# A four-layer convolution and state-space kernel: token stage under the kernel's own list schedule, side work on ScalarE, first convolution in three bf16 parts

## The chip, the cores and the metric

The kernel runs on one core of a Trainium2 chip. The time is that of the device in microseconds (us), the median of several runs. The profile is one execution taken by the hardware profiler. Engines are called PE (TensorE), DVE (VectorE), ACT (ScalarE), POOL (GpSimd) and SP (SyncE, which here only issues DMAs). All arithmetic is fp32 unless said otherwise.

## What is computed

The input x is 64 images of 128 channels and 28x28 pixels. Four layers follow each other; each works on the output of the one before:

```
# layer 0: quantised residual block
out = conv3x3(x, quant_weight(w1, 4))          # weights: integers -15..15, over 15
out = quant_act(batchnorm(out, gamma1, beta1), 4)
out = conv3x3(out, quant_weight(w2 * (mask2 > 0.5), 4))
x   = quant_act(batchnorm(out, gamma2, beta2) + x, 4)
# layer 1: self-attention over the 784 pixels of an image
x   = gamma * (softmax(q^T k) applied to v) + x
# layer 2: state-space scan over 784 steps (160 channels x 24 states), fused back, residual
x   = x + scale * (fusion_w @ mamba(layernorm(four scan directions of x)))
# layer 3: state-space scan over 8 tokens of 16 channels for each pixel (32 channels x 16 states)
seq = x.transpose(0, 2, 3, 1).reshape(B * H * W, 8, 16)
  xz = seq @ in_proj_w.T ; causal conv of width 4, silu -> xs ; B, C, dt from xs
  dt = softplus(dt * dt_proj_w + dt_proj_b)
  h  = exp(dt_t * A) * h + dt_t * B_t * xs_t ;  y_t = sum over 16 states of h * C_t
  out = ((y + xs * D) * silu(z)) @ out_proj_w.T
x   = x + silu(groupnorm(out, 4 groups))
```

Batch norm in layer 0 takes its mean and variance over all 64 images, so the first convolution must be finished before the second can start.

## The kernel before, in words

The work has three parts, one after the other, joined by tensors in DRAM.

**conv_block (lines 135 to 213)** runs the two convolutions. Weights are quantised once by `quantised` (line 147): `q1`, the first convolution's, as fp32, and `q2` as bf16. Then a loop over 32 groups of two images loads `xt` (line 177), and `conv3x3` (line 116) makes for each image and each half of it nine matmuls that accumulate in one PSUM bank, one for each tap of the 3x3 window (line 126). For the first convolution both operands are fp32. ACT copies the sums out (line 182), DVE takes batch statistics (line 184), and the result goes to DRAM. The second loop reads it back, quantises it to integers in bf16 (`qa`, line 199) and does the same with bf16 operands. These two loops are written in program order, and the framework's scheduler, which simulates the engines' time, orders the instructions of each engine.

**attention_and_mamba (from line 491)** does layers 1 and 2. It doesn't issue its instructions where they are written. A `Plan` (line 259) records each of them as a step, with the tiles it uses and the steps it must follow; a helper class makes one line, 472, issue all of them, so that in the profile they all have the line L472. `Plan.cost` (line 365) gives each step a price: for a matmul 0.06 + 0.0023 us per column, for POOL 0.2 + 0.0023 per element, for ACT 0.2 + 0.00093 per element, for DVE 0.14 + 0.00107 per element (tensor_scalar in SBUF 0.00053). POOL's steps, and those DVE steps that read two SBUF operands or are a tensor_scalar into SBUF, are marked as sharing one port, of which the planner lets one run at a time. `order` (line 392) is a list scheduler: it walks through simulated time and takes for each engine, among its first 32 ready steps, the first that can start within `patience` of the soonest. Steps recorded under `first()` get an earlier rank by `lead`. `issue` (line 466) tries twelve pairs of lead and patience, takes the order that ends first by its own prices, and issues it as a fixed order. Steps recorded under `together()` stay side by side.

**token_mamba (from line 1077)** does layer 3. Before the change it issues directly, and the framework's scheduler orders it. The 50,176 pixels are cut into 28 groups of 14x128; each group has two halves of 16 channels (`dh`), each half four blocks of four channels, so there are 224 blocks. For each:

- `x_proj` (once a group): matmuls L1192 and L1198 give B, C and dt; the pairs of columns are copied out of PSUM into `BC` at L1202; `small` holds dt and the sum over states of B*C (L1207 to L1216).
- `delta_u` (once a half): ACT makes `delta`, PE transposes `u`; softplus is built from ACT's Abs, Exp and Ln, with DVE's L1254 (w = e + 1), L1255 and L1256 and POOL's L1259 and L1260; L1263 makes `diag`.
- `exps` (once a block): 64 small ACT exponentials, 128x98 each, fill the tile `a` of one block. There are two such tiles.
- `block`: POOL makes `db` = u*B for each token (`inject`, L1293; five tiles), and L1304 and L1306; DVE carries the state `h` in PSUM over the tokens: L1305, then L1308 (h*a), L1310 (h*C, written over `a`, or into `late` for the last two tokens) and L1312 (h + db). PE sums over the 16 states with identity matmuls: L1315, L1317 (which reads `a`, and so frees it) and L1319. ACT copies the sum into `ysb`.
- `gate` (once a half): PE transposes back, L1335 adds D*u, L1336 multiplies by z on POOL, a DRAM tensor `ygd` holds the first half until the second is there, L1344 projects, L1354 copies into the image's tile `xr`.
- `finish_image` (once an image, 64 in all): group norm statistics (L1137, L1139), ten tiny operations on a 128x8 tile `sm` (L1143 to L1154, mostly on DVE, with an Ln and an Exp on ACT), a silu gate by three ACT operations, the affine xr at L1162 on DVE, and on POOL L1164 and L1165.

All ACT operations of this part that go through `tables.act` have the line L228. The driver loop at the end of the function interleaves the parts: in each block it advances the gate and finish steps of the half before by two, the next group's `x_proj` by two and the next half's `delta_u` by one, and issues the next block's exps ahead of the present block.

Of the kernel before, what the change touches and what calls it, by code (L numbers as in the profile page):

```python
# [16 lines left out]
F32 = mybir.dt.float32  # L17
# [98 lines left out]
def conv3x3(nc, ps, w, src):  # L116

    img = src.rearrange("p (h w) -> p h w", w=HW)
    taps = [(0, 0)] + [(dy, dx) for dy in (-1, 0, 1) for dx in (-1, 0, 1) if (dy, dx) != (0, 0)]
    for half in range(2):  # L120
        acc = ps[:, half, :HT].rearrange("p (h w) -> p h w", w=HW)
        r0 = half * 14
        for i, (dy, dx) in enumerate(taps):
            lo, hi = max(r0, -dy), min(r0 + 14, HW - dy)
            a, b = max(0, -dx), min(HW, HW - dx)
            nc.tensor.matmul(  # L126
                acc[:, lo - r0 : hi - r0, a:b],
                lhsT=w[:, (dy + 1) * 3 + dx + 1, :],
                rhs=img[:, lo + dy : hi + dy, a + dx : b + dx],
                start=(i == 0),  # L130
                stop=(i == len(taps) - 1),
            )


def conv_block(tc, cpool, dram, x, w1t, w2t, m2t, v, eps):
# [6 lines left out]
    with ExitStack() as ctx:  # L142
# [4 lines left out]
        def quantised(name, src, mask, dtype):  # L147
# [19 lines left out]
            q = wp.tile([C, 9, C], dtype, name=f"q{name}")  # L167
# [3 lines left out]
        q1 = quantised("1", w1t, None, F32)  # L171
        q2 = quantised("2", w2t, m2t, BF16)

        st1 = wp.tile([C, NB * 2, 6], F32, name="st1")
        for g in range(NB // GRP):
            xt = big.tile([C, GRP, T], F32, name="xt")
            nc.sync.dma_start(xt, x[g * GRP : (g + 1) * GRP].rearrange("b c t -> c b t"))
            raw = big.tile([C, GRP, T], F32, name="raw")
            for k in range(GRP):
                acc = ps.tile([C, 2, 512], F32, name="acc")  # L180
                conv3x3(nc, acc, q1, xt[:, k, :])
# [10 lines left out]
        for g in range(NB // GRP):  # L192
# [7 lines left out]
            for k in range(GRP):  # L200
                acc = ps.tile([C, 2, 512], F32, name="acc")
                conv3x3(nc, acc, q2, qa[:, k, :])
# [56 lines left out]
class Plan:  # L259
# [12 lines left out]
    def __init__(self, tc):  # L272
        self.tc = tc
# [91 lines left out]
    def cost(self, engine, method, outs, ins, args, kw):  # L365
# [5 lines left out]
        if engine == "tensor":  # L371
# [4 lines left out]
            return 0.06 + 0.0023 * n, False, 0.25  # L376
        if engine == "gpsimd":
            return 0.2 + 0.0023 * n, True, 0.07
# [112 lines left out]
def attention_and_mamba(tc, tables, x, c2d, s2, b2x15, x2d, utd, ztd, pk3, pk4, vec, v, ident, eps):  # L491
# [11 lines left out]
    with ExitStack() as ctx:  # L503
# [99 lines left out]
        plan = Plan(tc)  # L603
# [473 lines left out]
def token_mamba(tc, tables, x2d, utd, ztd, pk4, v, ident, eps, out, NB):  # L1077
# [17 lines left out]
    with ExitStack() as ctx:  # L1095
        dram = ctx.enter_context(dram)
        wp = ctx.enter_context(tc.tile_pool(name="w4", bufs=1))
# [3 lines left out]
        ap = ctx.enter_context(tc.tile_pool(name="a4", bufs=2))  # L1101
        p2 = ctx.enter_context(tc.tile_pool(name="p4", bufs=2))
        p1 = ctx.enter_context(tc.tile_pool(name="p4b", bufs=1))
        db = ctx.enter_context(tc.tile_pool(name="db4", bufs=5))
        cp = ctx.enter_context(tc.tile_pool(name="c4", bufs=4))
        xrp = ctx.enter_context(tc.tile_pool(name="xr4", bufs=4))
        ps = ctx.enter_context(tc.tile_pool(name="ps4", bufs=3, space=PSUM))
        psd = ctx.enter_context(tc.tile_pool(name="psd4", bufs=1, space=PSUM))
        psh = ctx.enter_context(tc.tile_pool(name="psh4", bufs=1, space=PSUM))
        psy = ctx.enter_context(tc.tile_pool(name="psy4", bufs=2, space=PSUM))  # L1110
# [13 lines left out]
        act = tables.act  # L1124
        act(A, w("Alog"), AF.Exp)
        nc.vector.tensor_scalar(A, A, -1.0, None, ALU.mult)

# [5 lines left out]
        def finish_image(b):  # L1133
            xo = xr.pop(b)
            stats = p2.tile([C, 2, 6], F32, name="stats")
            for h in range(2):
                nc.vector.bn_stats(stats[:, h, :], xo[:, h * HT : (h + 1) * HT])  # L1137
            mv = p2.tile([C, 2], F32, name="mv")
            nc.vector.bn_aggr(mv, stats.rearrange("p n s -> p (n s)"))  # L1139
            acc = bank()  # L1140
            nc.tensor.matmul(acc[:, 0:1], lhsT=grp, rhs=mv[:, 0:1], start=True, stop=True)
            sm = p2.tile([C, 8], F32, name="sm", bufs=4)
            nc.vector.tensor_copy(sm[:, 0:1], acc[:, 0:1])  # L1143
            nc.vector.tensor_sub(sm[:, 1:2], mv[:, 0:1], sm[:, 0:1])
            nc.vector.scalar_tensor_tensor(sm[:, 2:3], sm[:, 1:2], sm[:, 1:2], mv[:, 1:2], ALU.mult, ALU.add)
            acc2 = bank()
            nc.tensor.matmul(acc2[:, 0:1], lhsT=grp, rhs=sm[:, 2:3], start=True, stop=True)
            act(sm[:, 3:4], acc2[:, 0:1], AF.Ln, bias=eps)
            act(sm[:, 4:5], sm[:, 3:4], AF.Exp, scale=-0.5)
            nc.vector.tensor_mul(sm[:, 5:6], sm[:, 4:5], v("gn_gamma"))  # L1150
            nc.vector.tensor_mul(sm[:, 6:7], sm[:, 0:1], sm[:, 5:6])
            nc.vector.tensor_sub(sm[:, 7:8], v("gn_beta"), sm[:, 6:7])
            nc.vector.tensor_scalar(sm[:, 0:1], sm[:, 5:6], -1.0, None, ALU.mult)
            nc.vector.tensor_scalar(sm[:, 1:2], sm[:, 7:8], -1.0, None, ALU.mult)  # L1154
            res = p1.tile([C, T], F32, name="res")
            nc.sync.dma_start(res, x2d[b])

            e = p1.tile([C, T], F32, name="gate")
            act(e, xo, AF.Exp, bias=sm[:, 1:2], scale=sm[:, 0:1])
            act(e, e, AF.Ln, bias=1.0)  # L1160
            act(e, e, AF.Exp, scale=-1.0)
            nc.vector.tensor_scalar(xo, xo, sm[:, 5:6], sm[:, 7:8], ALU.mult, ALU.add)  # L1162
            yield
            nc.gpsimd.tensor_tensor(xo, xo, e, ALU.mult)  # L1164
            nc.gpsimd.tensor_tensor(res, res, xo, ALU.add)  # L1165
            nc.sync.dma_start(out[b], res)

        def load_rows(src, k, dh, g, n):
# [3 lines left out]
            for b in range(lo // T, (hi - 1) // T + 1):  # L1172
                p, q = max(lo, b * T), min(hi, (b + 1) * T)
                nc.sync.dma_start(t[:, p - lo : q - lo], src[b][:, dh, p - b * T : q - b * T])
# [4 lines left out]
        def x_proj(k):  # L1179
# [5 lines left out]
            for g, n in chunks:  # L1185
                uts = [load_rows(utd, k, dh, g, n) for dh in range(2)]
                for g2 in range(0, n, 2):
                    two = bank()
                    for j in range(2):
                        at = slice((g2 + j) * C, (g2 + j + 1) * C)  # L1190
# [308 lines left out]
```

## Time and profile before

| what | us |
|---|---|
| three runs | 14403.58, 14459.57, 14449.58 |
| median | 14449.58 |
| the profiled execution: own time | 14456.75 |
| the profiled execution: span | 14454.9 |
| granted TensorE clock, mean | 0.838 of full |
| busy in the span: PE, DVE, ACT, POOL | 10855.2, 12706.4, 10460.3, 11391.7 |
| first convolution, first to last product | 18.6 to 744.6 |
| second convolution | 755.3 to 944 |
| attention and first scan | 957 to 8060 |
| token stage | 8060 to 14455 |

The span is the time from the first to the last instruction of that execution. A group's row gives line, engine, operation, output and inputs, shapes, count, busy time, the mean of one in ns, and the engine's idle time just before it with what ended it. A row by tile gives least, median and largest duration in ns. A row of waits gives who waited for whom, the total in us, how often, and the longest. In the profile a busy engine may be waiting: an instruction is counted from its start to its end, whatever it does in between.

### The profile page before, as it was taken

The numbers are of one execution on the slowest core, as the hardware profiler recorded it, in microseconds if no ns is written. First come the engines' busy times: TensorE is split into PE (matmuls) and PEld (weight loads), VectorE is DVE, ScalarE is ACT, GpSimd is POOL, SyncE is SP. The second block draws the span as 40 slices with busy tenths as digits, with TensorE's granted clock in tenths as the row PEclk, the third lists the DMA queues.
The fourth block names the chain that finished last, engine by engine and source line by source line (L and its number), as shares of the span: only waits on it lengthen the run. The fifth ranks groups of instructions, "written<-read, shape, count | busy, mean of one in ns | idle before, by whom it ended". The sixth has DMA issues, their size and how long they took to land. (4 is left out here: it accounts for less than half of the span.)

```text
span 14454.9 us, 181149 instructions
## 1 busy us (share of the span) xinstructions
PE 10855.2 (75%) x58370; PEld 7180.2 (50%) x58370; DVE 12706.4 (88%) x13524; ACT 10460.3 (72%) x25236; POOL 11391.7 (79%) x5304
## 2 busy tenths in 40 slices
PE   9987777777777777777776676776767767677676
PEld 5654444444444444444443455555555555555554
DVE  1048999999999999999999799999999999999998
ACT  0047777777777777777777677777777777777776
POOL 0007899889898888889889788888888887888887
PEclk9988888888888888888887787888878888888787
DMA  2243444444444444444444211111112111111111
GB/s 74 72 162 109 135 123 128 129 121 127 131 121 126 130 120 124 133 122 124 134 121 125 67 45 46 55 48 52 45 48 60 44 49 47 49 59 42 49 50 44
DMA packets 711515, 1297.64 MB, mean 90 GB/s; under 512 B 206624, under 2 KB 357536, under 8 KB 710560
## 3 DMA queue, kind: packets, MB, share of 16 engines
q1 hardware_dynamic: 710560, 1286.05, 29.8%
q8 instruction: 460, 7.54, 0.2%
q14 instruction: 495, 4.06, 0.1%
HBM read 954.72 MB, written 330.76 MB: 89 GB/s over the span
## 5 line engine op out<-in xcount | busy, mean ns | idle before, releaser
L228 ACT ACTIVATE a<-delta,A 128x98 f32<-128x98 f32 x14336 | 3906.2, 365 | 1123.2 <-PE y L1317 827.4
L472 POOL TENSOR_TENSOR h<-ur,Br 128x784 f32<-128x784 f32 x1920 | 4205.3, 2216 | 152.6 <-PE y L472 136.3
L1293 POOL TENSOR_TENSOR db<-u,BC 128x896 f32<-128x896 f32 x1568 | 3274.0, 2101 | 856.0 <-DVE h L1312 688.1
L1317 PE MATMUL y<-a,ident 128*128 128x280 f32 x7168 | 2089.5, 455 | 954.2 <-DVE a L1310 898.5
L472 DVE TENSOR_TENSOR_SCAN ah<-ah,h 128x392 f32<-128x392 f32 x2304 | 2303.1, 1000 | 60.8 <-ACT ah L472 50.3
L1317 PEld LDWEIGHTS y<-a,ident 128*128 128x128 f32 x7168 | 1557.7, 221 | 1512.4 <-POOL db L1293 729.1
L472 DVE TENSOR_TENSOR_SCAN h<-a,h 128x784 f32<-128x784 f32 x768 | 1915.0, 2498 | 112.7 <-ACT a L472 57.9
L472 ACT ACTIVATE ah<-dr,A 128x392 f32<-128x392 f32 x2304 | 1322.9, 587 | 612.8 <-DVE ah L472 592.4
L472 POOL TENSOR_TENSOR h<-h,Cr 128x784 f32<-128x784 f32 x640 | 1350.7, 2114 | 357.9 <-DVE h L472 347.5
L1308 DVE TENSOR_TENSOR h<-h,a 128x896 f32<-128x896 f32 x1344 | 1473.7, 1096 | 33.1
L472 DVE TENSOR_TENSOR h<-ah,Cr 128x392 f32<-128x392 f32 x2304 | 1302.5, 565 | 72.9
L472 PE MATMUL y<-h,fold 128*32 128x98 f32 (+1 forms) x12288 | 1024.0, 422 | 385.2 <-DVE h L472 357.2
L1312 DVE TENSOR_TENSOR h<-h,db 128x896 f32<-128x896 f32 x1120 | 1228.2, 1097 | 59.1 <-POOL db L1293 0.5
L472 POOL TENSOR_TENSOR xn<-s,sq 128x784 f32<-128x784 f32 x64 | 136.5, 2133 | 1183.6 <-ACT sq L472 1142.9
L472 PEld LDWEIGHTS bank<-vt,et 112*112 112x112 f32 x6272 | 905.4, 215 | 233.9 <-ACT et L472 90.6
L1310 DVE TENSOR_TENSOR a<-h,BC 128x896 f32<-128x896 f32 x896 | 974.1, 1087 | 21.4
L472 PE MATMUL bank<-vt,et 112*112 112x128 f32 x6272 | 981.6, 320 | 5.0 <-ACT et L472 2.3
L1319 PE MATMUL y<-late,ident 128*128 128x112 f32 x7168 | 848.0, 275 | 14.3 <-DVE late L1310 13.4
L1319 PEld LDWEIGHTS y<-late,ident 128*128 128x128 f32 x7168 | 838.5, 193 | 37.8 <-DVE late L1310 18.0
L472 PEld LDWEIGHTS y<-h,fold 128*32 128x32 f32 x12288 | 378.8, 121 | 909.7 <-DVE h L472 428.8
L472 ACT ACTIVATE a<-dr,A 128x784 f32<-128x784 f32 x768 | 716.8, 942 | 152.0 <-DVE h L472 150.4
L126 PE MATMUL acc<-xt,q 128*128 128x378 f32 (+3 forms) x2304 | 726.0, 478 | 18.6 <-DVE q L168 18.6
(213 smaller groups left out, 20969.2 us busy)
## 6 DMA issues: line engine op xcount, KB each, us to landing
Br<-bcd SPq DMA_DIRECT2D x1536, 98.0 KB, 2.4
Cr<-bcd SPq DMA_DIRECT2D x1536, 98.0 KB, 2.4
dr<-dud SPq DMA_DIRECT2D x1280, 98.0 KB, 2.4
ur<-dud SPq DMA_DIRECT2D x1280, 98.0 KB, 2.3
utd<-tok SPq DMA_DIRECT2D x128, 392.0 KB, 2.7
ztd<-tok SPq DMA_DIRECT2D x128, 392.0 KB, 3.7
rows<-utd SPq DMA_DIRECT2D x192, 256.0 KB, 2.8
xt<-in_x SPq DMA_DIRECT2D x32, 784.0 KB, 5.2
```

What stands on the lines that cost most here:

```text
L126: nc.tensor.matmul(acc[:, lo - r0 : hi - r0, a:b], lhsT=w[:, (dy + 1) * 3 + dx + 1, :], rhs=img[:, lo + dy : hi + dy, a + dx : b + dx], st ...
L228: ins = self.tc.nc.scalar.activation(*args, **kw)
L472: last = getattr(getattr(nc, engine), method)(*args, **kw)
L1293: nc.gpsimd.tensor_tensor(x, of_dg(du[:, t, ds, :]), BC[:, t, :NS, :].unsqueeze(1).broadcast_to([C, DB, NS, G]), ALU.mult)
L1308: nc.vector.tensor_tensor(h, h, flat(at(t)), ALU.mult)
L1310: nc.vector.tensor_tensor(by_d(dst), h_d, Cc(t), ALU.mult)
L1312: nc.vector.tensor_tensor(h, h, flat(inject(t)), ALU.add)
L1317: nc.tensor.matmul(y3[:, 1:6], lhsT=ident, rhs=a[:, 0:5, :, n, :], start=False, stop=False)
L1319: nc.tensor.matmul(y3[:, 6:8], lhsT=ident, rhs=late[:, :, :, n, :], start=False, stop=(n == NS - 1))
```

## The change

Three edits are made together.

1. **First convolution.** `q1` is made in bf16 (its values are integers from -15 to 15). Each group's `xt` is split into three bf16 tiles whose sum is `xt`: a rounded copy on ACT, the remainder by a subtraction on DVE, its rounded copy on ACT, and the last remainder on DVE. `conv3x3` takes a list of images and adds one matmul for each of them at each tap; the second convolution passes a list of one.

2. **Token stage under a `Plan`.** Every instruction of the stage, except the preamble, is recorded in a plan of its own and issued by `plan.issue()` at the end. `Plan` gets two of its prices as arguments: us per matmul column and us per POOL element. The first scan's plan keeps 0.0023 and 0.0023; the token stage's has 0.0019 and 0.0021. The matmuls that accumulate in one bank and the exponentials in fours are kept together; each block and its `ysb` copy are recorded under `first()`.

3. **Side work.** In the token stage the `BC` copy (L1202) and w = e + 1 (L1254) go from DVE to ACT. The group norm's tiny operations all go to ACT in another form: Square of (mean of the channel less that of the group), add the variance, and after Ln and Exp three Identity operations for scale and shift. The affine of `xr` (L1162) goes to ACT and is written in place ahead of the gate's exponential, which then needs no scale and bias of its own.

```diff
-def conv3x3(nc, ps, w, src):
-    img = src.rearrange("p (h w) -> p h w", w=HW)
+def conv3x3(nc, ps, w, parts):
+    imgs = [m.rearrange("p (h w) -> p h w", w=HW) for m in parts]
...
-            nc.tensor.matmul(
-                acc[:, lo - r0 : hi - r0, a:b],
-                lhsT=w[:, (dy + 1) * 3 + dx + 1, :],
-                rhs=img[:, lo + dy : hi + dy, a + dx : b + dx],
-                start=(i == 0),
-                stop=(i == len(taps) - 1),
-            )
+            for img in imgs:
+                nc.tensor.matmul(
+                    acc[:, lo - r0 : hi - r0, a:b],
+                    lhsT=w[:, (dy + 1) * 3 + dx + 1, :],
+                    rhs=img[:, lo + dy : hi + dy, a + dx : b + dx],
+                    start=(i == 0 and img is imgs[0]),
+                    stop=(i == len(taps) - 1 and img is imgs[-1]),
+                )
...
-        q1 = quantised("1", w1t, None, F32)
-        q2 = quantised("2", w2t, m2t, BF16)
+        q1 = quantised("1", w1t, None)
+        q2 = quantised("2", w2t, m2t)
...
+            parts = [big.tile([C, GRP, T], BF16, name=f"part{i}") for i in range(3)]
+            nc.scalar.copy(parts[0], xt)
+            nc.vector.tensor_tensor(xt, xt, parts[0], ALU.subtract)
+            nc.scalar.copy(parts[1], xt)
+            nc.vector.tensor_tensor(parts[2], xt, parts[1], ALU.subtract)
...
-                conv3x3(nc, acc, q1, xt[:, k, :])
+                conv3x3(nc, acc, q1, [m[:, k, :] for m in parts])
...
-    def __init__(self, tc):
-        self.tc = tc
+    def __init__(self, tc, column, element):
+        self.tc, self.column, self.element = tc, column, element
...
-            return 0.06 + 0.0023 * n, False, 0.25
+            return 0.06 + self.column * n, False, 0.25
         if engine == "gpsimd":
-            return 0.2 + 0.0023 * n, True, 0.07
+            return 0.2 + self.element * n, True, 0.07
...
-        plan = Plan(tc)
+        plan = Plan(tc, 0.0023, 0.0023)
...
+        plan = Plan(tc, 0.0019, 0.0021)
...
-        ap = ctx.enter_context(tc.tile_pool(name="a4", bufs=2))
+        ap = plan.pool(ctx.enter_context(tc.tile_pool(name="a4", bufs=2)), 2)
...
-        act = tables.act
-        act(A, w("Alog"), AF.Exp)
+        tables.act(A, w("Alog"), AF.Exp)
         nc.vector.tensor_scalar(A, A, -1.0, None, ALU.mult)
+        act = plan.scalar.activation
...
-            sm = p2.tile([C, 8], F32, name="sm", bufs=4)
-            nc.vector.tensor_copy(sm[:, 0:1], acc[:, 0:1])
-            nc.vector.tensor_sub(sm[:, 1:2], mv[:, 0:1], sm[:, 0:1])
-            nc.vector.scalar_tensor_tensor(sm[:, 2:3], sm[:, 1:2], sm[:, 1:2], mv[:, 1:2], ALU.mult, ALU.add)
+            sm = p2.tile([C, 6], F32, name="sm", bufs=4)
+            act(sm[:, 0:1], acc[:, 0:1], AF.Square, bias=mv[:, 0:1], scale=-1.0)
+            act(sm[:, 1:2], sm[:, 0:1], AF.Identity, bias=mv[:, 1:2])
...
-            act(sm[:, 3:4], acc2[:, 0:1], AF.Ln, bias=eps)
-            act(sm[:, 4:5], sm[:, 3:4], AF.Exp, scale=-0.5)
-            nc.vector.tensor_mul(sm[:, 5:6], sm[:, 4:5], v("gn_gamma"))
-            nc.vector.tensor_mul(sm[:, 6:7], sm[:, 0:1], sm[:, 5:6])
-            nc.vector.tensor_sub(sm[:, 7:8], v("gn_beta"), sm[:, 6:7])
-            nc.vector.tensor_scalar(sm[:, 0:1], sm[:, 5:6], -1.0, None, ALU.mult)
-            nc.vector.tensor_scalar(sm[:, 1:2], sm[:, 7:8], -1.0, None, ALU.mult)
+            act(sm[:, 2:3], acc2[:, 0:1], AF.Ln, bias=eps)
+            act(sm[:, 2:3], sm[:, 2:3], AF.Exp, scale=-0.5)
+            act(sm[:, 3:4], v("gn_gamma"), AF.Identity, scale=sm[:, 2:3])
+            act(sm[:, 4:5], acc[:, 0:1], AF.Identity, scale=sm[:, 3:4])
+            act(sm[:, 5:6], sm[:, 4:5], AF.Identity, bias=v("gn_beta"), scale=-1.0)
...
-            act(e, xo, AF.Exp, bias=sm[:, 1:2], scale=sm[:, 0:1])
+            act(xo, xo, AF.Identity, bias=sm[:, 5:6], scale=sm[:, 3:4])
+            act(e, xo, AF.Exp, scale=-1.0)
             act(e, e, AF.Ln, bias=1.0)
             act(e, e, AF.Exp, scale=-1.0)
-            nc.vector.tensor_scalar(xo, xo, sm[:, 5:6], sm[:, 7:8], ALU.mult, ALU.add)
...
-                    nc.vector.tensor_copy(
-                        BCf[:, :, g + g2 : g + g2 + 2], two.rearrange("p (c j) -> p c j", j=2)
-                    )
+                    act(BCf[:, :, g + g2 : g + g2 + 2], two.rearrange("p (c j) -> p c j", j=2), AF.Copy)
...
-            nc.vector.tensor_scalar(w_, e_, 1.0, None, ALU.add)
+            act(w_, e_, AF.Identity, bias=1.0)
...
-                for n in range(NS):
-                    col = (dh * ND + i * DB + d) * NS + n
-                    act(a[:, :, d, n, :], delta[:, 1:, i * DB + d, :], AF.Exp, scale=A[:, col : col + 1])
+                for n0 in range(0, NS, 4):
+                    with plan.together():
+                        for n in range(n0, n0 + 4):
+                            col = (dh * ND + i * DB + d) * NS + n
+                            act(a[:, :, d, n, :], delta[:, 1:, i * DB + d, :], AF.Exp, scale=A[:, col : col + 1])
...
-                y, dst = block(k, dh, i, a, ysb)
-                act(dst, y, AF.Copy)
+                with plan.first():
+                    y, dst = block(k, dh, i, a, ysb)
+                    act(dst, y, AF.Copy)
...
         for _ in ends:
             pass
+        plan.issue()
```

In the lines of the token stage that are not shown, `nc.` becomes `plan.` (`nc.vector.tensor_tensor` becomes `plan.vector.tensor_tensor`, and so on for all five engines), the pools are wrapped like `ap`, and runs of matmuls into one bank are put under `plan.together()`.

## The prediction

> **What bounds the kernel now.** I read the time by stage first, from the answer by windows: the two convolutions, attention with the first scan, and the token stage (last line), with the token stage's steady part above it. Columns after the length are busy us and instructions of PE, PE weight load, DVE, ACT and POOL, then TensorE's granted clock, DMA share and GB/s.
>
> ```profile
> 18.60:744.60 726.00, 726.00 (x2304) 439.03 (x2304) 68.41 (x130) 51.18 (x63) 0.00 (x0) 1.00 0.22 69
> 755.30:944.00 188.70, 188.38 (x1152) 112.72 (x1152) 122.61 (x188) 100.65 (x94) 0.00 (x0) 0.99 0.75 257
> 1120.00:8060.00 6940.00, 5363.20 (x33152) 3017.04 (x33143) 6627.54 (x7350) 5359.50 (x8742) 6191.44 (x2811) 0.85 0.42 125
> 8150.00:14400.00 6250.00, 4354.00 (x20718) 3453.12 (x20719) 5772.08 (x5633) 4798.03 (x16073) 5159.38 (x2467) 0.81 0.17 49
> 8060.00:14455.00 6395.00, 4449.66 (x21148) 3525.62 (x21148) 5824.16 (x5715) 4857.88 (x16193) 5187.98 (x2480) 0.81 0.17 49
> ```
>
> The first convolution is TensorE alone: busy without a gap at clock 1.00. In the token stage DVE is busy 5772 of 6250 us (92.4%). Part of that is not work. From the view by tile (least/median/most ns) and the timeline (start, us):
>
> ```profile
> L1293 POOL TENSOR_TENSOR db<-u,BC x1568: 1908/1940/3824, 8144.9 to 14389.3; 128x896 f32<-128x896 f32 x196
> L1304 POOL TENSOR_TENSOR a<-a,db x224: 2065/2086/3862, 8160.4 to 14380.6; 128x896 f32<-128x896 f32 x112
> L1305 DVE TENSOR_TENSOR h<-a,db x224: 1073/1577/6776, 8162.5 to 14382.7; 128x896 f32<-128x896 f32 x112
> ...
> L1254 DVE TENSOR_SCALAR w<-e x56: 1075/2817/4815, 8131.2 to 14199.7; 128x1792 f32<-128x1792 f32 x56
> ```
> ```profile
> 10011.23 1.95 POOL L1293 TENSOR_TENSOR db<-u,BC 128x896 f32<-128x896 f32 x1
> 10012.09 2.97 DVE L1209 TENSOR_TENSOR w<-BC 128x1792 f32<-128x1792 f32 x1
> ```
>
> L1254 costs 1.08 us alone and 2.8 at the median. L1209 is 2.0 us at its least; here it is recorded from 10012.09, but POOL's instruction ends at 10013.18, and 10013.18 + 2.0 is where L1209 ends plus 0.1. So some DVE operations are billed for waiting until POOL is through; those with one operand in PSUM (L1308, L1310, L1312, 1.09 us with hardly any spread) are not. The waits say what else is late:
>
> ```profile
> ACT a L228 <- PE y L1317: 827.4, 137, 19.9
> ```
> ```profile
> POOL db L1293 <- DVE h L1312: 688.1, 418, 6.0
> ```
>
> ACT waits for the sums on TensorE that free one of two a tiles; POOL, five db tiles ahead, waits for DVE.
>
> **What the Trainium skill says.** "SBUF — State Buffer", section "SBUF: two separate sides": VectorE and GpSimd have one port pair as an exclusive lock for a whole instruction, and VectorE needs it for two SBUF inputs or its two-port modes. The trace agrees (the pair above). "FP8 and Floating Point Precision", section "TensorE Precision Notes": true fp32 is four passes. The trace agrees: 726.0/1152 = 0.630 us per fp32 product against 188.4/1152 = 0.1635 in bf16, 3.9 times. "ScalarE: Activation LUTs", section "What ACT_TABLE_LOAD costs": 186 ns + 0.833 ns per element, about 93 more per pointer operand. The gate rows agree: 1.036 us with two pointers, 0.845 without.
>
> **Part 1, first convolution in three bf16 parts.** Out: 1152 fp32 products, 726 us. In: 3456 bf16 products of the same columns. At conv 2's 0.1635 us: 565 us; gain 161. Weight loads double as beside conv 2 (98 ns each, under 164), so they stay hidden. Added per two images: two ACT copies at 1.69 (L196, the same 1568 elements) and two DVE subtractions; a 1792-element two-input op is 2.01 at least, so 1568 take 1.77. All 32 groups: ACT +108 us, DVE +113; ACT comes to 159 and DVE to 181 in 565, POOL is idle, so they hide under 17.7 us of TensorE per group, three buffers deep. Were that cover gone it would cost 7 us a group. An ACT copy that waits for its xt holds back the copies of finished sums queued behind it, and TensorE waits for those; four PSUM tiles of 8.8 us each cover that, so nothing. At the start the four steps queue beside the weight quantisation on DVE (first product at 18.6): 0 to 7 us, I take 4. Bounds: the clock holds over 189 us of bf16; over 565 it is unshown. At the 0.85 of the next stage conv 1 takes 665: gain 57. Range +55 to +165, taken **157**. Conv 2 and the first scan are unchanged (the planner's numbers there stay 0.0023).
>
> **Part 2, side work off VectorE.** Recorded DVE time that goes, from the groups: L1202 133.7 (196 copies), L1254 129.1, L1162 78.2, the eight sm lines L1143 to L1154 228.1: 569 us, which leaves 5255. Only part is work. Waiting in it: L1254 129-56x1.075 = 69, L1162 78-64x0.673 = 35, five two-input sm lines 200-48 = 152: 256.
> ACT gains: 196 BC copies at 0.605 (the like u copy; if the pairs cost as the strided r copy against a plain one, 682 to 489, 0.85), 119 to 166; 56 of w at 1.69, 95; per image one affine 1.04 less 0.19 (the exp loses its pointers) and five small ones at 0.22 (the sm rows are 0.25 and 0.19), x64 = 124. ACT goes from 4858 to 5196. A BC bank is then freed by ACT, with exps queued ahead of it: x_proj on TensorE waits for the bank, and the next group's inject for BC. x_proj is recorded a whole half (four blocks) before the scan that reads BC, so I cost it at nothing; without that lead a copy stuck behind one tile of exps (64x0.272 = 17.4 us; the chain has 25 in 6.79) would cost 17.4x28 = 490 us. The sm chain (ACT now waits 95 us for it) no longer crosses DVE, but Square and Ln wait on ACT for two small matmuls, 0.25 us each, with exps behind them.
>
> **Part 3, the order.** No arithmetic changes otherwise; the same DMAs go through SP by the plan. SP's loads (rows six tiles deep) are covered by 0.17 DMA use; without cover the 51.6+44.7+35.2 us of TensorE waits on rows and yg would grow. What limits the stage after part 2 is the lock. POOL alone, medians: 1568x1.94 + 448x2.09 + 112x3.99 + yg 260 + 128x1.85 = 4922. DVE operations that need it, at their least: L1305 240, L1255/6 225, L1263 112, L1209 56, and those that go (60+43+48 = 151). Before: 4922+784 = 5706 in 6250, 91%. After: **5555**, 24.8 us for each of 224 blocks, against DVE 5255/224 = 23.5 and ACT 23.2. The ring of a is near: exps 17.4, L1304 to t=5 some 18, sums 9 to 11, about 47 for two blocks, so 23.5 per block. So the lock, DVE, ACT and the ring lie within 7%, and the lock is the highest.
> How full can an order keep the lock? The first scan, already in this planner, keeps its limiting engine at 6627.5/6940 = 95.5%. The same here: 5555/0.955 = 5817 steady, plus 145 of start and tail as now: 5962, against 6395: **gain 433**. Bounds: a full lock, 5555+145, gain 695; the present 91%, 5555/0.913+145 = 6229, gain 166.
>
> **Sum** against the profiled execution (14456.75 us, span 14454.9; 0.05% over the median of the three runs, 14449.58): 14457-157-433 = 13867 us.
>
> **Rivals.**
> *The planner fills better.* DVE keeps its 92.4%, now of 5203 steady: 5631+145, gain 619; 14457-619-157 = 13681. For it: the planner's prices (0.2+0.0021 per element: 2.08 for 1.94 measured) lie above POOL's. Against: the lock would be 98.7% full.
> *The order is worth nothing.* Three engines and a lock drift against any fixed order, the lock stays at 91%: 14457-166-157 = 14134. For it: DVE already idles only 478 us in the steady part.
> *The change doesn't do what it says in conv 1*: gain 57, and the rest as forecast: 13967.
> *Slower: ACT becomes the bound.* In-order ACT now idles 6395-4858 = 1537 us, 827 of it for a tiles. If a plan with heavier ACT keeps those waits, the stage is 5196+1537 = 6733, +338: 14457+338-157 = 14638. It decides once ACT's idle time per block stays over (6395+157-5196)/224 = 6.1 us (now 6.9). Against: the sm chain's 95 us go, and L1305, which starts each block's chain to the sums, has fewer DVE operations ahead of it, so the a tiles come free earlier.
>
> **Chances.** Forecast 0.57; better filling 0.17; order worth nothing 0.14; conv 1 short 0.07; ACT bound 0.05. The likeliest's own range, lock 92 to 98%, is 13760 to 14020. To hold 8 in 10 I reach to 13600 (full lock, conv gain 157) and 14140 (no gain by order). Half a per cent, 72 us, is what a measurement can tell from no change: faster 0.94, same 0.02, slower 0.04.
>
> **What would show it.** Conv 1's window near 565 us with TensorE still gapless and clock 1.00; token stage near 5960 us; DVE about 88% busy there and ACT 87%; L1254's and sm's DVE rows gone; L1305's median still above 1.07 us; ACT's wait for the y sums cut to half or less. Wrong if POOL's idle time stays near 1200 us, if ACT has over 6 us idle per block, or if conv 1's clock falls.

## The result and the profile after

| kernel | median us | lowest to highest | runs |
|---|---|---|---|
| before | 14450.95 | 14403.58 to 14459.57 | 4 |
| after | 14120.24 | 14110.18 to 14121.71 | 4 |

The ratio is 0.9776, 95% interval 0.9755 to 0.9798: 331 us less, where 583 had been forecast (14449.58 to 13867). The span of the profiled execution is 14117.3 us, the mean granted clock 0.84 as before.

In the changed kernel all instructions of the token stage come from the plan's one issuing line, L480, so they are told apart by tile. The answer by windows of the changed kernel (columns as in the prediction): first convolution, token stage, and its steady part. The token stage is counted here from the start of the last activation of the preceding step, an instruction that both kernels have, to the end of the span.

```profile
18.60:586.40 567.80, 564.79 (x3456) 338.14 (x3456) 177.92 (x194) 138.89 (x125) 0.00 (x0) 1.00 0.25 90
7920.10:14117.30 6197.20, 4448.37 (x21088) 3543.16 (x21088) 5420.43 (x4873) 5183.68 (x16808) 5098.32 (x2480) 0.82 0.17 50
7981.00:14062.00 6081.00, 4378.72 (x20774) 3488.98 (x20774) 5394.22 (x4840) 5123.04 (x16663) 5063.55 (x2463) 0.82 0.17 50
```

The kernel before in the same view, from the same instruction:

```profile
8089.10:14454.90 6365.80, 4430.34 (x21088) 3516.85 (x21088) 5816.71 (x5701) 4843.37 (x16172) 5187.98 (x2480) 0.81 0.17 49
```

The token stage starts 8089.1-7920.1 = 169 us earlier: 158 of that are the first convolution (726.0 to 567.8). Its own length falls from 6365.8 to 6197.2, again **169 us**, where the prediction had 433. The lock demand of the prediction, 5555 us, over the steady 6081 is 91.3%: the share of before (5706 of 6250), not 95.5%. DVE's busy time falls by 396 us but its idle time (length less busy) grows from 549 to 777: more than half of what it was relieved of came back as idle time.

By tile (least/median/most ns), the rows that answer to those of before; the third was L1305, the fourth, now on ACT, L1254; the last is L1256:

```profile
L480 POOL TENSOR_TENSOR db<-u,BC x1568: 1908/1939/3789, 7969.6 to 14055.6; 128x896 f32<-128x896 f32 x196
L480 POOL TENSOR_TENSOR a<-a,db x224: 2067/2085/3862, 7983.0 to 14046.9; 128x896 f32<-128x896 f32 x112
L480 DVE TENSOR_TENSOR h<-a,db x224: 1072/1966/5185, 7985.1 to 14049.0; 128x896 f32<-128x896 f32 x112
L480 ACT ACTIVATE w<-e x56: 1681/1697/1700, 7955.1 to 13893.6; 128x1792 f32<-128x1792 f32 x56
L480 DVE SCALAR_TENSOR_TENSOR delta<-delta,e x56: 2024/3638/3801, 7958.9 to 13925.2; 128x1792 f32<-128x1792 f32 x56
```

On ACT, w costs 1.70 us with hardly any spread, so no wait shows in it. On DVE the rows that still need the lock wait somewhat longer in sum. The row on delta shows it: its median was 2.754 us and is 3.638, with nearly the same least. The largest row, h<-a,db, does not, though its median rose from 1.577 to 1.966 us: its mean fell. The groups, before and after (busy us, then mean ns of one):

```profile
L1305 DVE TENSOR_TENSOR h<-a,db 128x896 f32<-128x896 f32 x224 | 461.2, 2059 | 161.2 <-POOL a L1304 151.7
L1256 DVE SCALAR_TENSOR_TENSOR delta<-delta,e 128x1792 f32<-128x1792 f32 x56 | 147.6, 2636 | 0.1
```
```profile
L480 DVE TENSOR_TENSOR h<-a,db 128x896 f32<-128x896 f32 x224 | 434.6, 1940 | 128.4 <-POOL db L480 89.1 <-POOL a L480 37.8
L480 DVE SCALAR_TENSOR_TENSOR delta<-delta,e 128x1792 f32<-128x1792 f32 x56 | 170.2, 3040 | 1.9
```

The waits of the kernel before, where the prediction does not show them, and those of the changed kernel:

```profile
DVE yg L1335 <- PE bank L1330: 45.0, 27, 7.4
...
PE y L1315 <- ACT ysb L228: 334.2, 96, 5.6
```

```profile
DVE yg L480 <- PE bank L480: 204.8, 30, 13.6
DVE h L480 <- POOL db L480: 169.6, 71, 5.7
...
ACT a L480 <- PE y L480: 837.4, 174, 9.0
POOL db L480 <- DVE h L480: 95.7, 103, 2.0
...
PE y L480 <- ACT ysb L480: 615.2, 161, 6.6
```

POOL's wait for DVE at db, 688.1 us before, has nearly gone; but POOL's idle time fell only from 1178 to 1099 us, and it now waits elsewhere. ACT's wait for the sums has not moved (827.4 before; in run 1 below, whose token stage is that of before, it is 725.1, so this figure is good to some 100 us). TensorE's wait for ACT's copy of the sums has almost doubled. DVE's wait for a TensorE bank in the gate step (yg) was 45.0 and is 204.8. The timeline of the changed kernel shows one such case (start, us, engine; in brackets how long the engine stood idle before, and for whom):

```profile
10045.25 3.72 PE L480 MATMUL y<-late,ident 128*128 128x112 f32 x32
10046.54 6.04 ACT L480 ACTIVATE delta<-small,pk 128x112 f32<-128x112 f32 x16
...
10052.48 3.30 ACT L480 ACTIVATE a<-delta,A 128x98 f32<-128x98 f32 x12
...
10055.68 0.52 ACT L480 ACTIVATE ysb<-y 128x448 f32<-128x448 f32 x1
...
10056.25 1.98 PE L480 MATMUL bank<-ident,ysb 128*128 128x128 f32 x8 [6.63 <-ACT ysb L480]
...
10057.42 0.75 DVE L480 SCALAR_TENSOR_TENSOR yg<-rows,vec,bank 128x512 f32<-128x512 f32 x1 [9.66 <-PE bank L480]
```

The sums are complete at 10048.97. The copy that passes them on lies in ACT's fixed order behind 16 instructions for the next half and 12 exponentials, and starts 6.7 us later. After a few transposes TensorE's next instruction needs the copy, and DVE's next needs TensorE: one engine's fixed order has stopped two others.

### The profile page after: what moved, and what is told of

Read it like the earlier page. It is cut to its first block, busy times and chain, and to the rows that moved or that the text cites. A ratio compares the mean times of both kernels' runs of the same rounds, so it can differ in the third digit from the quotient of the medians.

```text
span 14117.3 us, 184013 instructions
## 1 busy us (share of the span) xinstructions
PE 10708.4 (76%) x59522; PEld 7094.5 (50%) x59522; DVE 12411.9 (88%) x12760; ACT 10892.9 (77%) x25936; POOL 11304.5 (80%) x5304
## 5 line engine op out<-in xcount | busy, mean ns | idle before, releaser
L480 ACT ACTIVATE a<-delta,A 128x98 f32<-128x98 f32 x14336 | 3901.3, 366 | 899.3 <-PE y L480 837.4
L480 POOL TENSOR_TENSOR h<-ur,Br 128x784 f32<-128x784 f32 x1920 | 4206.4, 2216 | 156.0 <-PE y L480 140.7
L480 POOL TENSOR_TENSOR db<-u,BC 128x896 f32<-128x896 f32 x1568 | 3201.6, 2069 | 96.9 <-DVE h L480 95.7
L480 PE MATMUL y<-a,ident 128*128 128x280 f32 x7168 | 2087.9, 457 | 567.1 <-DVE a L480 560.4
L480 DVE TENSOR_TENSOR_SCAN ah<-ah,h 128x392 f32<-128x392 f32 x2304 | 2305.0, 1000 | 63.5 <-ACT ah L480 50.5
L480 PEld LDWEIGHTS y<-a,ident 128*128 128x128 f32 x7168 | 1566.9, 222 | 1118.9 <-POOL u L480 227.1
L480 DVE TENSOR_TENSOR_SCAN h<-a,h 128x784 f32<-128x784 f32 x768 | 1903.9, 2483 | 118.6 <-ACT a L480 60.1
L480 ACT ACTIVATE ah<-dr,A 128x392 f32<-128x392 f32 x2304 | 1323.1, 587 | 611.8 <-DVE ah L480 592.0
L480 POOL TENSOR_TENSOR h<-h,Cr 128x784 f32<-128x784 f32 x640 | 1350.0, 2113 | 356.3 <-DVE h L480 337.3
L480 DVE TENSOR_TENSOR h<-h,a 128x896 f32<-128x896 f32 x1344 | 1476.9, 1099 | 44.6
L480 DVE TENSOR_TENSOR h<-h,db 128x896 f32<-128x896 f32 x1120 | 1231.4, 1099 | 179.5 <-POOL db L480 80.5
L480 DVE TENSOR_TENSOR h<-ah,Cr 128x392 f32<-128x392 f32 x2304 | 1303.7, 566 | 72.8
L480 PE MATMUL y<-h,fold 128*32 128x98 f32 (+1 forms) x12288 | 1030.9, 424 | 381.6 <-DVE h L480 354.9
L480 PEld LDWEIGHTS bank<-vt,et 112*112 112x112 f32 x6272 | 891.8, 212 | 234.8 <-ACT et L480 91.9
L480 DVE TENSOR_TENSOR a<-h,BC 128x896 f32<-128x896 f32 x896 | 976.9, 1090 | 27.8
L480 PE MATMUL bank<-vt,et 112*112 112x128 f32 x6272 | 968.4, 317 | 6.0 <-ACT et L480 2.8
L480 POOL TENSOR_TENSOR xn<-s,sq 128x784 f32<-128x784 f32 x64 | 136.3, 2130 | 1016.1 <-ACT sq L480 968.3
L480 PEld LDWEIGHTS y<-late,ident 128*128 128x128 f32 x7168 | 835.3, 192 | 30.7 <-issue 11.2
L480 PEld LDWEIGHTS y<-h,fold 128*32 128x32 f32 x12288 | 381.7, 121 | 909.1 <-DVE h L480 424.6
L480 ACT ACTIVATE a<-dr,A 128x784 f32<-128x784 f32 x768 | 716.9, 942 | 151.9 <-DVE h L480 147.2
L480 PE MATMUL y<-late,ident 128*128 128x112 f32 x7168 | 833.3, 274 | 0.0
L480 PE MATMUL y<-diag,ident 128*128 128x448 f32 x448 | 358.9, 900 | 615.2 <-ACT ysb L480 615.2
```

Source lines behind the costliest of these rows:

```text
L480: last = getattr(getattr(nc, engine), method)(*args, **kw)
```

## The experiments

The kernels of runs 1 to 4 ran on one chip, 5 to 8 on another, 9 to 11 on a third and 12 on a fourth, each beside the kernel before, whose medians were 14441.5, 14434.9, 14434.2 and 14447.7. Each has 4 runs, and a ratio to the kernel before with its 95% interval. Where a plan is used, an edit also makes the planner choose another order; how much that alone can do is seen in runs 4, 8 and 10. Unless a kernel leaves something out, it computes the whole.

**1. The convolution alone** (the kernel before, with the three parts in the first convolution).

> The kernel before with the first convolution in three bf16 parts and nothing else. Both theories: conv 1 from 726 to 567 us, the rest unchanged, so 14451 - 158 = 14293 us. If it is far from that, part of the stage times of the changed kernel comes from the convolution too.

14295.8 us, ratio 0.9898 [0.9883, 0.9913]. That is 146 us less, within the interval of what was forecast, 157. The rest of the difference between the two kernels, some 176 us, belongs to the token stage.

**2. Convolution and side work, no plan** (the changed kernel; a class in the place of `Plan` passes each instruction on at once, so that the framework's scheduler orders the stage as before).

```diff
-        plan = Plan(tc, 0.0019, 0.0021)
+        plan = Direct(tc, tables)
```

> The changed kernel with its token stage issued directly (ordered by the framework's scheduler, as before), side work on ScalarE. Theory A (the port lock of VectorE and GpSimd limits the stage, and every order fills it to 91%): lock demand 5555 as in the changed kernel, stage 6226, so about 14120 us. Theory B (ScalarE and TensorE wait for each other through the a and y tiles, and only the planner's order bears the heavier ScalarE): stage 6395 or more, 14290 us or more.

14051.1 us, ratio 0.9731 [0.9716, 0.9745]: 245 us below run 1 and some 69 below the change itself. Both expectations missed: the moved work needs no new order, and it is worth more than the prediction's bound of 166 us for it. The stage's window in this kernel, and the waits that had been the ones to watch:

```profile
7930.10:14068.00 6137.90, 4396.01 (x21088) 3485.29 (x21088) 5332.51 (x4873) 5130.78 (x16808) 5260.89 (x2480) 0.81 0.18 51
```
```profile
ACT a L235 <- PE y L1351: 455.1, 100, 13.6
POOL db L1326 <- DVE h L1345: 531.3, 359, 5.9
...
DVE h L1338 <- POOL a L1337: 358.9, 102, 13.6
```

Here ACT's wait for the sums does fall to about half, as the prediction had it of the plan. But DVE, 484 us less busy than in the kernel before, gives 256 of them back as idle time, mostly in waits for POOL (h<-a,db waited 151.7 us before).

**3. Convolution and plan, side work on DVE** (the changed kernel with the BC copies, w, sm and the affine as before).

```diff
-                    act(BCf[:, :, g + g2 : g + g2 + 2], two.rearrange("p (c j) -> p c j", j=2), AF.Copy)
+                    plan.vector.tensor_copy(BCf[:, :, g + g2 : g + g2 + 2], two.rearrange("p (c j) -> p c j", j=2))
...
-            act(w_, e_, AF.Identity, bias=1.0)
+            plan.vector.tensor_scalar(w_, e_, 1.0, None, ALU.add)
```

> The changed kernel with the side work back on VectorE, still under the plan. Theory A: lock demand 5706 again, 5706/0.9135 + 145 = 6391 for the stage, so about 14285 us. Theory B: ScalarE is 340 us lighter and the order is kept, so no slower than the changed kernel: 14050 to 14130 us.

14212.7 us, ratio 0.9838 [0.9822, 0.9854]: 83 us below run 1, between both expectations. The order by itself is worth something while DVE still has its side work. In the window DVE is busy 5771 of 6300 us:

```profile
7911.90:14211.50 6299.60, 4377.88 (x21088) 3539.00 (x21088) 5770.67 (x5701) 4860.85 (x16172) 5025.14 (x2480) 0.82 0.17 50
```

**4. The change with the first scan's prices.**

```diff
-        plan = Plan(tc, 0.0019, 0.0021)
+        plan = Plan(tc, 0.0023, 0.0023)
```

> The changed kernel with the planner's old prices (0.0023 and 0.0023) in the token stage. Theory A: the lock is filled to 91% by this order too, 14120 us within 40. Theory B (the order matters, and so do its prices): the planner believes GpSimd 9% slower than it measures, 14200 us or more.

14052.9 us, ratio 0.9731 [0.9716, 0.9745]: 67 us faster than the change, and as fast as run 2, with no plan. Both expectations missed. So on top of the side work the plan brings nothing at these prices, and costs 67 to 69 us at its own. The window, and the wait at the gate step:

```profile
7921.50:14056.60 6135.10, 4315.62 (x21088) 3462.51 (x21088) 5360.75 (x4873) 5189.05 (x16808) 5160.13 (x2480) 0.82 0.18 51
```
```profile
DVE yg L480 <- PE bank L480: 103.1, 25, 9.4
```

DVE has less to wait for at the gate step, but more elsewhere: its idle time is 774 us, for 777 in the change. The 62 us by which the stage is shorter are in its busy time, 5361 us for 5420, and there in lock waits: added up as durations less the least of their row, they come to some 296 us for 368.

**5. Load off the lock.** POOL's product with C for token 1 is left out (the only product with C on POOL; the others are DVE's): 224 instructions of 2.09 us, 468 us of the lock.

```diff
-            plan.gpsimd.tensor_tensor(by_d(at(1)), by_d(at(1)), Cc(1), ALU.mult)
```

> The changed kernel without GpSimd's product of token 1 with C (one 2.09 us instruction a block; token 1's term is left out of y in its C factor). VectorE's chain doesn't wait for it. Theory A (the port lock limits the stage, filled to 91%): demand 5555 - 468 = 5087, stage 5087/0.9135 + 145 = 5714 against 6226, so 14120 - 512 = 13610 us. Theory B (ScalarE and TensorE, bound to each other through the a and y tiles, set the pace): under 100 us of gain, 14020 us or more.

14067.0 us, ratio 0.9739 [0.9724, 0.9755]: 53 us below the change. If the lock were the limit, over 500 would have to go. The demand is now 5555-468 = 5087 in a steady part of 6142.2-116 = 6026 us (116 as in the change): 84% full. POOL's busy time falls by 290 us only, since its other instructions are recorded longer, and it waits for DVE instead:

```profile
7914.80:14057.00 6142.20, 4391.86 (x21088) 3506.28 (x21088) 5448.05 (x4873) 5187.09 (x16808) 4808.49 (x2256) 0.82 0.18 51
```
```profile
POOL db L480 <- DVE h L480: 691.7, 486, 5.3
```

**6. Load off ACT.** Two states at a time share one decay rate, so that a block needs 32 exponentials of 196 elements in place of 64 of 98; the rates of every second state are left out.

```diff
-                        for n in range(n0, n0 + 4):
+                        for n in range(n0, n0 + 4, 2):
...
-                            act(a[:, :, d, n, :], delta[:, 1:, i * DB + d, :], AF.Exp, scale=A[:, col : col + 1])
+                            act(
+                                a[:, :, d, n : n + 2, :],
+                                delta[:, 1:, i * DB + d, :].unsqueeze(2).broadcast_to([C, NK - 1, 2, G]),
+                                AF.Exp, scale=A[:, col : col + 1],
+                            )
```

> The changed kernel with the exponentials of two states made by one ScalarE instruction of twice the length (both states take the first one's decay rate): 32 instead of 64 a block, some 6 us a block less on ScalarE, all waits and tiles as before. Theory A: ScalarE is not the limit, 14060 to 14180 us. Theory B: the ring of the a tiles gets 6 of 47 us shorter for two blocks and ScalarE 1370 us lighter, stage 300 us shorter or more, 13820 us or less.

14022.4 us, ratio 0.9714 [0.969, 0.9737]: 98 us below the change, between both expectations, though ACT has 1302 us less to do (window, and the wait that took its place, 837.4 in the change):

```profile
7923.00:14009.40 6086.40, 4362.94 (x21088) 3505.78 (x21088) 5413.11 (x4873) 3881.35 (x9640) 5126.04 (x2480) 0.84 0.18 51
```
```profile
ACT a L480 <- PE y L480: 1359.6, 139, 19.3
```

**7. The same product moved instead of left out.** Token 1's product with C goes to DVE, which takes one operand from PSUM. DVE's products of this kind show no lock wait here (1.080 to 1.094 us, all 1120 of them).

```diff
-            plan.gpsimd.tensor_tensor(by_d(at(1)), by_d(at(1)), Cc(1), ALU.mult)
+            plan.vector.tensor_tensor(by_d(at(1)), h_d, Cc(1), ALU.mult)
```

> The changed kernel with the product of token 1 with C on VectorE from the state in PSUM (1.09 us, no lock) in place of GpSimd from SBUF (2.09 us of lock). Theory A: lock demand 5087, VectorE's own work up by 244 us to about 5300 with 370 of waits; VectorE is then the limit, at 95% busy about 5970 for the stage, 13870 us. Theory B: VectorE's chain of a block gets 1.1 us longer and the sums later, no gain: 14100 us or more.

14135.1 us, ratio 0.9784 [0.9767, 0.98]: no difference from the change that can be told from noise. POOL's busy time falls to 4758 us, DVE's rises to 5614 of 6206, and POOL waits 754 us for DVE.

**8. Prices as the trace has them.** The planner's prices for POOL and ACT in the token stage are set to the durations of the profile (db 1.98 us, exps 0.272, other POOL 0.22 + 0.00212 per element, other ACT 0.19 + 0.00083).

```diff
+            if self.measured:
+                return (1.98 if outs[0].tensor.name.startswith("db") else 0.22 + 0.00212 * n), True, 0.07
...
+                if n == 98:
+                    return 0.272, False, 0.07
...
```

> The changed kernel with the planner's prices for ScalarE and GpSimd set to the durations in its own trace (exponentials 0.272 instead of 0.291 us, db 1.98 instead of 2.08, others within 0.05). Theory A: every order fills the lock to 91 to 93%, so 14040 to 14130 us. Theory C (the fixed order loses because its prices are wrong): the forecast's stage of 5960 us, 13860 us.

14202.1 us, ratio 0.9834 [0.9818, 0.9849]: 82 us slower than the change. Both expectations missed. Of three sets of prices the one nearest to the trace gives the slowest order: 14053, 14120, 14202 us. The gate step waits longest here:

```profile
DVE yg L487 <- PE bank L487: 293.6, 53, 20.7
```

**9. Load off DVE.** DVE's product with C for token 2 is left out: 224 instructions of 1.09 us, 244 us or some 250 with the gaps between them, none of it lock.

```diff
-                plan.vector.tensor_tensor(by_d(dst), h_d, Cc(t), ALU.mult)
+                if t != 2:
+                    plan.vector.tensor_tensor(by_d(dst), h_d, Cc(t), ALU.mult)
```

> The changed kernel without VectorE's product of token 2 with C (1.09 us a block, no lock; token 2's term is left out of y in its C factor). GpSimd's lock and ScalarE's work were worth 54 of 468 us and 98 of 1370. Theory D (VectorE's in-order queue limits the stage: own work, lock waits, gaps, and the waits for TensorE between them): the whole 1.09 us and its gap of 0.05 are won, 224 x 1.14 = 255 us, 13865 us. Theory B (the ring through the a and y tiles): only half of it, one block's 1.1 us of a ring of two blocks, 13990 us. Theory A (lock): nothing, 14120 us.

13981.1 us, ratio 0.9694 [0.9679, 0.9708]: 139 us below the change, a little over half of what was taken away. That is close to what Theory B named. DVE is then busy 5081 of 6078 us (84%), so it isn't the limit by itself either. It waits longer at the gate step than in run 8, in a faster kernel:

```profile
7941.40:14019.60 6078.20, 4378.10 (x21088) 3509.60 (x21088) 5080.61 (x4649) 5185.94 (x16808) 5044.08 (x2480) 0.83 0.18 51
```
```profile
DVE yg L480 <- PE bank L480: 326.0, 56, 14.4
```

**10. Another order.** Of the planner's twelve pairs of lead and patience, only the one that ends last by its own prices is used.

```diff
         plan = Plan(tc, 0.0019, 0.0021)
+        plan.TRIED = [(0, 0.12)]
```

> The changed kernel with the token stage's order fixed to lead 0 and patience 0.12, the one that the planner holds for the worst of its twelve by its own estimate. Theory P (the planner's choice by its own prices is a guide): slower by over 100 us, 14220 us or more. Theory Q (differences between its orders are drift that its prices don't see, as the old and the measured prices suggest, 14053 and 14202 us): 14040 to 14200 us, no order among them.

14311.3 us, ratio 0.9916 [0.99, 0.9933]: 191 us slower than the change, with the same work. Within one set of prices the planner's estimate did tell the worst order from the best one; the orders between were not run.

**11. More side work to ACT** (run 2, with the copies into `xr` and `small` on ACT too).

```diff
-                        plan.vector.tensor_copy(xr[b][:, o : o + c], acc[:, at - lo : at - lo + c])
+                        act(xr[b][:, o : o + c], acc[:, at - lo : at - lo + c], AF.Copy)
...
```

> The version with the side work on ScalarE and no plan (14051 us), with VectorE's last copies out of TensorE's sums (xr and small, 228 instructions, some 95 us of VectorE and 11 of gaps) on ScalarE too, which gets 110 us. Theory D: VectorE's 106 us are won, 13945 us. Theory B (ScalarE in the ring): ScalarE gets heavier and its in-order queue later, 14051 us or more.

14080.5 us, ratio 0.9755 [0.9741, 0.977]: not faster than run 2 (0.9731). DVE is busy 5256 us, 77 less, ACT 64 more, and DVE gains a wait for ACT's copies:

```profile
DVE stats L1169 <- ACT xr L235: 111.4, 49, 8.3
```

**12. Two loads off at once** (run 5 and run 6 together; leaves out what both leave out).

> Both reliefs of no_c1 and exps_pairs at once (ScalarE 1300 us lighter, 468 us off the lock; token 1's C factor is left out and pairs of states share a decay rate); VectorE's work is that of the changed kernel. Alone they won 54 and 98 us. Theory E (VectorE, the lock and ScalarE are near-limits that cover one another, so that relief of one is mostly eaten by the next): together they win far more than their sum; VectorE, busy 5420 us, is left as the limit at the 91 to 95% that it reached before, stage 5700 to 5950, 13620 to 13870 us. Theory F (VectorE's chain and its waits for TensorE's in-order queue set the stage, the other two hardly matter): the sum of the two, 13970 us, or less of a gain.

13712.6 us, ratio 0.9493 [0.9476, 0.951]: 408 us below the change, as Theory E had it, where the two alone gave 53+98 = 151. The relief of the lock that won 53 us by itself wins 310 beside the relief of ACT (run 6 to run 12). Window and waits:

```profile
7936.00:13720.50 5784.50, 4319.93 (x21088) 3479.53 (x21088) 5422.05 (x4873) 3874.63 (x9640) 4722.18 (x2256) 0.84 0.19 54
```
```profile
DVE yg L480 <- PE bank L480: 45.3, 28, 8.4
...
ACT a L480 <- PE y L480: 1472.0, 174, 15.8
```

DVE does the same work as in the change (5422 us), but in 5784.5 us: 93.7% busy. Only now is one engine close to full, though some 371 us of that are lock waits, as in the change; its waits for TensorE together have gone from 329 to 80 us. The mean granted clock of the stage is 0.84 here and in run 6, and 0.82 in the change; TensorE's busy time is 128 us (here) and 85 us (run 6) below that of the change. What that is worth was not tested; it can hardly be what divides run 12 from run 6.

## Why the prediction was right or wrong

The forecast of a faster kernel, the range and the sizes of the instructions held. The gain of the token stage did not, and 14120 us lies only 20 inside the slow end of the range, 14140.

**Part 1: right.** 158 us by the windows, 146 by the medians of run 1, for 157. 564.79/3456 = 0.1634 us per product at clock 1.00 for the whole 568 us, and 3.0 us of gaps in the first 6 us. ACT's share came to 139 us and DVE's to 178 (forecast 159 and 181), all of it hidden.

**Part 2: the instructions right, DVE's relief and its worth wrong.** ACT's busy time rose by 340 us (forecast 338). The BC copies did not hold TensorE up for long: 62.9 us of waits for them. But DVE's busy time fell by 396, not 569. There are two reasons. The groups' sums that I took the 569 from count overlapping time twice: before, they add up to 6014 us on DVE, where the engine is busy 5817, and after to 5499 for 5420. They fall by 515 us, and 119 of that was overlap. The other 54 us are longer durations of rows that stay, mostly lock waits. Taken as recorded less least in the rows with two inputs in SBUF, and the tensor_scalar rows that went, these were some 582 us before and are some 368 now. So 214 went, where I had let 256 go with the lines: the rows that stay lost 26 us at h<-a,db and gained 70 at the four others. As for the worth, my bound without help from an order was 166 us; run 2 against run 1 gives 245.

**Part 3: the step that failed is "How full can an order keep the lock?"** I took one of four loads, each within 7% of the others by my own list, for a single limit, and gave it the 95.5% that the limiting engine of the first scan reaches. So I took 5962 us for a stage that I counted as 6395. Three things in the runs speak against this. The share of the lock stayed at 91.3%. Taking 8% of the load off it (run 5) took 53 us and not 512, and its share fell to 84%. And the order, which was to bring 267 of the 433 us, brings nothing beside the side work (run 4 against run 2) or costs 69 us (the change against run 2); 83 us is what it brings where DVE still has all its work (run 3 against run 1).

What stands in its place: DVE, the lock with POOL, and ACT with its two tiles of `a` are full to 84 to 91% each, and they pass work to each other through TensorE. Take one load off, and the others take much or nearly all of the gain: 53 us won for 468 on the lock, 98 for 1302 on ACT, 139 for some 250 on DVE, nothing for a move from POOL to DVE. Off two at once, 408. That the loads of the lock and of ACT cover one another is shown by run 12: 257 us more than the sum of runs 5 and 6. Each single figure has the order's own scatter in it; the planner's chosen orders of the same work differ by up to 149 us (runs 4 and 8). How they cover one another, each engine's fixed order being late for another, is read from the waits and not tested by itself. In the change it can be seen at work: DVE, 396 us less busy, was idle 228 us longer, above all waiting for TensorE, 191 to 329, and TensorE there for ACT's copies.

The view that one looks at first, the engine with the highest occupancy, was of half a use: the Trainium skill, "Perfetto Trace Analysis", section "Identifying the Most-Contended Engine", says to optimise that engine first. It was DVE, 91% in the stage before, and taking work off it did pay (runs 2 and 9, not run 11). But some 580 us of its occupancy were waiting for the lock, and a little over half of what run 9 took off it showed in the time.

**The rivals.** "The order is worth nothing" named 14134 us, and 14120 came, with the share of the lock that it names. Its sum is nearly right for a reason that isn't: the side work was worth 245 us and not 166, and the order, at its prices, gave 69 of them back. The slower rival, ACT as the bound, did not come: ACT idles (6197-5184)/224 = 4.5 us per block, under the 6.1 from which it decides. The better filling did not come, and conv 1 was not short. The likeliest case's own range has an error of arithmetic in it: a lock filled to 92 to 98% gives 14088 to 13718 us by the prediction's own sum, not 14020 to 13760; the measured time is outside both.

**What was to show it.** As listed: conv 1's window, the rows that go, h<-a,db above 1.07 us, DVE 87.5% busy. Not as listed: a stage near 5960 us, ACT 83.6% busy where 87% was named, and a wait for the sums cut to half. POOL's idle time, 6197-5098 = 1099 us, was not clearly below the 1200 that would make the forecast wrong; of the signs of being wrong, it was the one that came near.

**What stays open.** Why the prices 0.0023 give a better order than truer ones. The gate step's wait goes with the time in run 4, the change and run 8 (103, 205, 294 us), but that is not the explanation of run 4, whose gain lies in lock waits, and run 9 is faster with 326. Nothing was run that changes that wait alone. A third bank for the sums, or their copy on DVE, would test how much the chain from sums to copy costs, and a third tile of `a` whether the ring through the two tiles sets the pace: that rival, Theory B of the expectations, named runs 5, 7, 9 and 11 right and missed in runs 2, 3, 4 and 6. None of these was tried. The fastest kernels that compute the whole are runs 2 and 4, at a ratio of 0.9731; both beat the change.

## What to carry to other kernels

Where several engines of a stage stand within some 10% of each other, don't price a relief by the fullest of them alone: much of it can go to the next, and here only two reliefs together showed what each is worth. Try a move of work without the new order, and the new order without the move, before believing in either; here the move alone did all of it, and more. The planner's estimate told two orders apart under one set of prices; prices nearer to the trace did not make a faster program.

## What the runs showed of the hardware that was not expected

- Lock waits recorded as busy time don't vanish with the lines that show them. With w gone to ACT, the two-input row on delta takes 3.64 us at the median for 2.02 at the least; before, it was 2.75 for 2.01. In all, the rows that stay gained 44 us of the 256 that had been counted as going.
- A bf16 stage kept the full granted clock for 568 us, three times as long as the trace of before could show.
- Half as many exponentials of twice the length save 1302 us in 7168 instructions, 0.182 us each: close to the fixed 186 ns that the prediction quoted for an ACT instruction. These have a pointer operand, which the prediction prices at 93 ns more; but an exponential is recorded at 0.364 us and adds only 0.272 to the busy time, so some 0.092 us of each overlap with the next, and the two nearly cancel.
